# Two layers on one core: sums of squares and block products handed to GpSimd and ScalarE, new places and buffers in layer 0

## The chip, the core and the metric

The kernel runs on one core of a Trainium2 chip. The core has five engines with queues of their own: TensorE (PE, matrix products and transposes, results in PSUM), VectorE (DVE), ScalarE (ACT), GpSimd (POOL) and SyncE (SP, which issues DMAs; POOL issues DMAs too, the indirect ones among them). Each engine takes its instructions in order, and one that waits for a semaphore holds up all that stand behind it in its queue. The metric is the device time of one execution in microseconds, the median of several.

## What is computed

Two transformer layers over x of shape 8 x 512 x 256 in float32, each with a modulated LayerNorm, attention, a second LayerNorm and a mixture of experts. Layer 0's attention is a recurrence over time, and its experts take one of eight by argmax. Cut to what the change touches:

```python
def _L0_attn_ref(x, Wq, Wk, Wv, Wo, Wbeta, rms_weight):
    q = _l2_normalize(silu(x @ Wq.T).reshape(B, S, N, H))      # 16 heads of 16
    k = _l2_normalize(silu(x @ Wk.T).reshape(B, S, N, H))
    v = silu(x @ Wv.T).reshape(B, S, N, H)
    beta = jax.nn.sigmoid(x @ Wbeta.T)
    def step(M, inp):
        q_t, k_t, v_t, b_t = inp
        out_t = jnp.einsum('bnh,bnhd->bnd', q_t, M)
        retrieved = jnp.einsum('bnhd,bnd->bnh', M, k_t)
        M = M + b_t[..., None, None] * jnp.einsum('bnh,bnd->bnhd', k_t, v_t - retrieved)
        return (M, out_t)
    ...                                                          # scan over the 512 steps
    out = out / rms * rms_weight
    return out @ Wo.T

def _L0_ffn_ref(x, gate_w, gate_b, expert_bias, w1, b1, w2, b2):
    top_idx = jnp.argmax(gate_logits, axis=-1)
    for e in range(NUM_EXPERTS):
        h = jax.nn.relu(x @ w1[e] + b1[e])
        out = out + (top_idx == e) * (h @ w2[e] + b2[e])

h = _layernorm(x) * (1 + ca) + sa
x = x + ga * _L0_attn_ref(h, ...)
h = _layernorm(x) * (1 + cb) + sb
x = x + gb * _L0_ffn_ref(h, ...)
...                                # layer 1: softmax attention with a bias, dense weighted experts
```

## The kernel before

The 512 times are cut into four tiles of 128 (`NT`); a tile holds 128 times of all eight batches, with time on the partitions, 256 values a batch.

**Layer 0.** `scan(i, K, V)` runs the recurrence of tile i on VectorE, 128 steps one after the other, with the 8 x 16 states on the partitions and 16 x 16 of M along the row. A step is four dependent operations: product L625, reduction L629, outer product L635, subtraction L640; every eight steps come L621 and L631. It yields after each step. `run(pieces, steps)` sorts pieces of other work by a place, a number, and issues each when the scan has come to the step of that number; pieces with a place behind the last step, and all pieces when no scan runs, are issued in the order of their places. `tc.issue_after(step)` puts the instructions of a piece behind that step on VectorE's queue; the other engines get them in the order in which they are issued.

Three kinds of work run beside scan s:

- `front(s+1)`, from place 47 on (30 in scan 0): `stats`, `normal`, `turn`, `project` for each batch, where ScalarE writes q, k, v, beta and the squares of q and k (L533); `squares` sums them in groups of 16 (L537, VectorE); per half of the batches `roots` (ScalarE takes square roots of the sums, L550) and `scales` (VectorE from L554, then the products L572, POOL); `heads` turns k and v for the scan.
- `attend(s-1)`, from place 0 on: per batch `turn`, `scores`, `mask` (POOL, L725), `weigh`, `state`, `project`. `state` takes the batch's part of the state for the next tiles out of PSUM, zeroed outside the heads' blocks by a product with `block` on VectorE (L797 for tile 0, L800 for later ones), and adds it (L801, POOL). Per half come `roots` (L804, VectorE), `rest` (scaling on ScalarE, L808, product and sum on POOL, L811 and L812, and the store of x1, L813) and `stats` (L820).
- `follow(s-1)` adds the routing and the experts of that tile. `route` is a generator of six pieces at places 38, 47, 56, 61, 63, 65: it normalises the rows in place (L870), turns them, makes the logits (L893, added to the bias in L908), turns them back into the same rows (`h[b]`), counts rows by expert (L928, L933, L940, L948) and ends with `slot` and `idx` (L980) and eight scatters to `hs` by indirect DMA (L984). `experts` has 15 slots of 128 rows, each of two halves: weights by indirect DMA on POOL (L1005, two buffers per part), rows `hslot` from `hs`, first product L1032, ReLU L1041, second product L1050, the bias L1056, and the store L1057 to `ys`. The first ten or twelve slots are issued behind place 73 of the same scan (`late`, `pace`); the rest go by `starts` into the next scan, or, for tile 2, into the tail. Then `gather` fetches each batch's rows of `ys` (L1065), multiplies them by the gate (L1094) and adds them to x in DRAM (L1095, an accumulating DMA), through the rotating buffers `yrow` (two).

After scan 3 comes the tail: the rest of tile 2's slots, the attention and routing of tile 3, the gathers of tiles 0 and 1, then tile 3's fifteen slots one every ten places (the list `last`), with the gathers of tile 2 and pieces of layer 1's `prologue` between them at places 102 + 4k (L261 are its products for q and k). `place1` makes layer 1's buffers first, with two memsets on VectorE.

**Layer 1** follows: softmax attention (L1243 to L1290) and dense experts (L1402 to L1418).

Pool tags matter: tiles of one tag share its buffers, and a new tile waits for the readers of the old one. `terms`, `upd` and `K` belong to the scan, `dm` to `state`, `qT` (two buffers) is shared by `attend`'s q and by the squares.

Of the kernel before, what the change touches and what calls it, by code (L numbers as in the profile page):

```python
# [19 lines left out]
P = 128  # L20
B = 8
# [42 lines left out]
def tile_two_layers(ctx: ExitStack, tc: tile.TileContext, t: dict, out: bass.AP):  # L64
# [217 lines left out]
    with ExitStack() as l0:  # L282
# [167 lines left out]
        def front(i, at):  # L450
# [83 lines left out]
                got["sq", b] = sq  # L534

            def squares(b):
                nc.vector.tensor_reduce(  # L537
                    ss[:, :, b, :], got["sq", b].rearrange("p s (n d) -> p s n d", d=HD),
                    AX.X, ALU.add,
                )  # L540


            n = B if i == 0 else B // 2
# [98 lines left out]
        def attend(i, qk, V, x1, norms):  # L642
# [149 lines left out]
            def state(b):  # L792
                pm = got["pm", b]
                pmv = pm[:, :D].rearrange("p (g m) -> p g m", g=2)
                blocks = block.unsqueeze(1).to_broadcast([P, 2, P])
                if i == 0:
                    nc.vector.tensor_mul(bdM[:, b], pmv, blocks)  # L797
                else:
                    dm = ap.tile([P, 2, P], F32, tag="dm", name=f"dm{i}_{b}")
                    nc.vector.tensor_mul(dm, pmv, blocks)  # L800
                    nc.gpsimd.tensor_add(bdM[:, b], bdM[:, b], dm)  # L801

            def roots(h):
# [42 lines left out]
        def route(i, h, norms):  # L846
# [12 lines left out]
                return x.unsqueeze(1).to_broadcast([P, n, x.shape[1]])  # L859

            lg = grid("lg")
            for half in range(2):
                rs, off = scale_offset(fp, "f", *norms[half])
                pl = bank()
                turned = None
                for n in range(5):
                    b = 4 * half + n
                    if n < 4:
                        hb = h[b]
                        nc.scalar.activation(  # L870
                            hb, hb, AF.Identity, bias=off[:, n : n + 1], scale=rs[:, n : n + 1]
                        )
                        pt = bank()
                        for c in range(2):
                            nc.tensor.transpose(
                                pt[:, c * P : (c + 1) * P], hb[:, c * P : (c + 1) * P], ident
                            )
                        hT = fp.tile([P, 2, P], F32, tag="hTf", name=f"hTf{i}_{b}", bufs=2)
                        for c in range(2):
                            by, plus = scale[0][:, 1, c, b : b + 1], shift[0][:, 1, c, b : b + 1]  # L880
                            if i == NT - 1 and c == 1:
                                nc.vector.tensor_scalar(
                                    hT[:, c, :], pt[:, c * P : (c + 1) * P], by, plus,
                                    ALU.mult, ALU.add,
                                )
                            else:
                                nc.scalar.activation(
                                    hT[:, c, :], pt[:, c * P : (c + 1) * P], AF.Identity,
                                    bias=plus, scale=by,
                                )  # L890
                    if n > 0:
# [8 lines left out]
                                back[:, c * P : (c + 1) * P], turned[:, c, :], ident  # L900
                            )
                        if i == NT - 1:
                            nc.vector.tensor_copy(h[b - 1], back[:, :D])
                        else:
                            nc.scalar.copy(h[b - 1], back[:, :D])
                    turned = hT
                yield
                nc.vector.tensor_add(  # L908
# [83 lines left out]
        def experts(i, slot, idx):  # L992
# [79 lines left out]
            if i == NT - 1:  # L1072
# [9 lines left out]
                        nc.gpsimd.dma_start(x2d[b][i], rows[b], accum_op=ALU.add)  # L1082
                yield
                return
            queue = []
            for b in range(B + 1):
                if b < B:
                    yr = fp.tile([P, D], F32, tag="yrow", name=f"yrow{i}_{b}", bufs=2)
                    with tc.issue_after(issued["scatter" if i == NT - 2 else "fetch"]):
                        gather(b, yr)  # L1090
                    queue.append(yr)
                if b > 0:
                    yr = queue.pop(0)
                    nc.gpsimd.tensor_mul(yr, yr, gates[1][:, b - 1, :])  # L1094
                    nc.gpsimd.dma_start(x2d[b - 1][i], yr, accum_op=ALU.add)  # L1095
                yield

        def follow(i, qk, V):
# [16 lines left out]
            def on():  # L1115
                next(work["experts"])

            pieces += [(38, begin), (47, more), (56, more), (61, more), (63, more), (65, settle)]

            late, pace, starts = {  # L1120
                NT - 1: (0, 4, [10 * j for j in range(NSLOT)]),
                NT - 2: (12, 4.3, [58, 68, 71]),
                NT - 3: (10, 4.6, [10, 26, 44, 50, 66]),
            }.get(i, (10, 4.6, [10, 26, 42, 58, 70]))
            rest = []
            for j in range(NSLOT):
                for half in range(2):
                    if j < late:
                        pieces.append((73 + pace * (j + half / 2), on))
                    else:  # L1130
                        rest.append((starts[j - late] + 3 * half, on))
# [438 lines left out]
```

## Time and profile before

Three runs: 2272.21 us median, 2269.37 to 2276.05. The profiled execution took 2273.54 us, its span is 2271.8.

| engine | busy, us | share of the span |
|---|---|---|
| PE | 1747.4 | 77% |
| DVE | 1602.2 | 71% |
| ACT | 1063.0 | 47% |
| POOL | 646.9 | 28% |

| stretch, us of the span | what runs | length, us |
|---|---|---|
| 0 to 65 | loads, front of tile 0 | 65 |
| 65.2 to 319.4 | scan 0 | 254.1 |
| 321.2 to 587.2 | scan 1 | 266.0 |
| 589.1 to 867.7 | scan 2 | 278.6 |
| 869.6 to 1120.6 | scan 3 | 251.0 |
| 1120.6 to 1404 | tail of layer 0 | 283 |
| 1404 to 2272 | layer 1 | 868 |

The scans are cut at their first and last VectorE operation. The shares of busy time over the span say little here, since each stretch has its own full engine. The chain of waits on the profile's page covers only layer 1, so that the stretches before it have to be read from the slices, from windows over each of them and from the waits of the engine that is full there. A line of a group has line, engine and operation, tiles and shapes, the count, busy time, mean duration in ns, and the idle time before these instructions with what ended it. A line of waits has the waiting instruction, what released it, the sum in us, how many times and the longest. A line of windows has the window, then busy time and number of instructions for each engine named in the header, the granted clock, DMA's share and GB/s.

### The profile page before, as it was taken

How to read it: one execution, taken by the hardware profiler on the slowest of the kernel's cores; microseconds unless marked ns; L12 is line 12 of the kernel's file. 1: busy time of each engine (PE TensorE's matmuls, PEld its weight loads, DVE VectorE, ACT ScalarE, POOL GpSimd, SP SyncE). 2: the span in 40 equal slices, each digit the busy share in tenths (PEclk: the TensorE clock that was granted, in tenths of full speed). 3: DMA queues.
4: the chain of work that ended last, by engine and by line, in shares of the span. 5: the costliest groups of instructions: out<-in, count | busy, mean ns of one | idle time of the engine just before them, and what ended most of it. 6: DMA issues, size and time to landing. Idle time of an engine off the chain costs nothing. (4 is left out here: it accounts for less than half of the span.)

```text
span 2271.8 us, 32168 instructions
## 1 busy us (share of the span) xinstructions
PE 1747.4 (77%) x10874; PEld 1204.0 (53%) x10874; DVE 1602.2 (71%) x4609; ACT 1063.0 (47%) x2571; POOL 646.9 (28%) x795
## 2 busy tenths in 40 slices
PE   5233026669687896869796787899999999999997
PEld 3212024448566685658775676555555555555553
DVE  3899999889997899999653001676676767666654
ACT  5144024554355543533332233878475666647431
POOL 1102016144472544743326643000102011110111
PEclk9667567689887998979997899899999999999998
DMA  5110000167313583238956884100101010100001
GB/s 160 47 44 9 0 1 10 36 214 278 142 54 98 198 292 121 80 110 317 268 120 162 278 309 141 42 8 15 19 15 24 15 27 12 24 13 13 17 17 17
DMA packets 88628, 214.11 MB, mean 94 GB/s; under 512 B 10872, under 2 KB 64288, under 8 KB 72848
## 3 DMA queue, kind: packets, MB, share of 16 engines
q0 software_dynamic: 33696, 161.98, 22.3%
q1 hardware_dynamic: 54768, 50.09, 7.6%
q8 instruction: 86, 1.41, 0.3%
q14 instruction: 78, 0.64, 0.1%
HBM read 175.10 MB, written 36.93 MB: 93 GB/s over the span
## 5 line engine op out<-in xcount | busy, mean ns | idle before, releaser
L1257 ACT ACTIVATE pr<-sc,low 128x384 f32<-128x384 f32 (+3 forms) x512 | 255.6, 556 | 196.5 <-DVE low L1252 194.2
L1032 PE MATMUL ps<-hTs,w 128*128 128x128 f32 x1920 | 250.7, 293 | 47.6 <-ACT hTs L1024 32.9
L1252 DVE CUSTOM_DVE_ANT_0 sc<-ps,strips 128x384 f32<-128x384 f32 (+3 forms) x512 | 225.4, 485 | 86.7 <-PE ps L1243 55.0
L1032 PEld LDWEIGHTS ps<-hTs,w 128*128 128x128 f32 x1920 | 239.2, 206 | 62.0 <-ACT hTs L1024 48.1
L629 DVE TENSOR_REDUCE state<-terms 128x16 f32<-128x272 f32 x512 | 227.3, 444 | 15.5
L1050 PE MATMUL ps<-w,act 128*128 128x256 f32 x960 | 223.3, 387 | 15.4 <-DMA w<-in_wrows,idx 12.6
L1408 PE MATMUL ps<-ew,hTd 128*128 128x512 f32 x512 | 232.9, 608 | 0.0
L640 DVE TENSOR_TENSOR state<-state,upd 128x256 f32<-128x256 f32 x511 | 220.6, 432 | 17.2
L635 DVE TENSOR_TENSOR upd<-K,state 128x256 f32<-128x256 f32 x511 | 213.9, 419 | 14.9
L1041 ACT ACTIVATE act<-ps,w 128x128 f32<-128x128 f32 x480 | 137.2, 369 | 186.1 <-PE ps L1032 104.7
L625 DVE TENSOR_TENSOR terms<-state,K 128x256 f32<-128x256 f32 x512 | 214.6, 419 | 11.9
L1050 PEld LDWEIGHTS ps<-w,act 128*128 128x128 f32 x960 | 182.1, 194 | 41.1 <-issue 13.9
L1269 PE MATMUL ps<-cst,pr 128*128 128x128 f32 x1280 | 191.5, 295 | 15.2 <-DVE low L1252 12.9
L1413 DVE SCALAR_TENSOR_TENSOR accd<-ps,wtd,accd 128x256 f32<-128x256 f32 x256 | 123.7, 483 | 101.4 <-PE ps L1408 89.5
L1269 PEld LDWEIGHTS ps<-cst,pr 128*128 128x128 f32 x1280 | 149.0, 148 | 83.9 <-DVE low L1252 24.7
L1417 POOL TENSOR_TENSOR accd<-accd,bc_g 128x256 f32<-128x256 f32 x32 | 23.2, 725 | 563.7 <-DVE accd L1413 563.7
L1408 PEld LDWEIGHTS ps<-ew,hTd 128*128 128x128 f32 x512 | 96.4, 193 | 121.2 <-issue 107.6
L1005 POOL DMA_INDIRECT w<-in_wrows,idx x120 | 117.3, 977 | 122.8 <-ACT act L1041 89.7
L1243 PE MATMUL ps<-kT,qTc 32*128 32x384 f32 (+3 forms) x1024 | 131.5, 492 | 6.3 <-DVE low L1252 4.4
L1278 DVE COPY prT<-ps 128x512 f32<-128x512 f32 (+3 forms) x256 | 117.0, 484 | 10.3 <-PE ps L1269 9.9
L725 POOL TENSOR_TENSOR stk<-stk,cst 128x512 f32<-128x512 f32 x96 | 119.3, 1270 | 17.1 <-ACT stk L724 15.1
L1276 ACT COPY prT<-ps 128x512 f32<-128x512 f32 (+3 forms) x256 | 99.0, 414 | 8.6 <-PE ps L1269 8.2
(252 smaller groups left out, 2878.7 us busy)
## 6 DMA issues: line engine op xcount, KB each, us to landing
hs<-zero SPq DMA_DIRECT2D x4, 1920.0 KB
hslot<-hs SPq DMA_DIRECT2D x60, 128.0 KB
ys<-ysb POOLq DMA_DIRECT2D x60, 128.0 KB, 3.1
x<-in_x SPq DMA_DIRECT2D x32, 128.0 KB
strips<-strip_d SPq DMA_DIRECT2D x16, 256.0 KB
out<-accd POOLq DMA_DIRECT2D x32, 128.0 KB, 3.1
wm<-in_wmod SPq DMA_DIRECT2D x4, 768.0 KB
xt<-in_x SPq DMA_DIRECT2D x12, 256.0 KB
```

The lines of the kernel that those rows point to most:

```text
L625: nc.vector.tensor_mul(term[:, :, :HD], M, K[:, s, :].unsqueeze(1).to_broadcast([P, HD, HD]))
L629: nc.vector.tensor_reduce(delta, term, AX.X, ALU.add)
L635: nc.vector.tensor_mul(upd, K[:, s, :].unsqueeze(2).to_broadcast([P, HD, HD]), delta.unsqueeze(1).to_broadcast([P, HD, HD]),)
L640: yield nc.vector.tensor_sub(M, M, upd).ins
L1032: nc.tensor.matmul(ph[:, q * P : (q + 1) * P], w[:, k * FF + f * P : k * FF + (f + 1) * P], hT[:, k, :], start=(k == 0), stop=(k == 1),)
L1041: nc.scalar.activation(act[:, f, :], ph[:, q * P : (q + 1) * P], AF.Relu, bias=w[:, 2 * FF + f : 2 * FF + f + 1],)
L1050: nc.tensor.matmul(py[:, :D], act[:, f, :], w[:, f * D : (f + 1) * D], start=(f == 0), stop=(f == NFC - 1),)
L1243: made = nc.tensor.matmul(pscs[r][:, :W], qT[rows, g, o, i * P : (i + 1) * P], kT[rows, g, :W], start=True, stop=True,)
L1252: nc.vector.tensor_tensor_reduce(out=sc[:, :W], in0=pscs[r][:, :W], in1=strips[:, n, S - W :], scale=1.0, scalar=3.0e38, op0=ALU.add, op1= ...
L1257: nc.scalar.activation(pr, sc[:, :W], AF.Exp, bias=low, scale=-1.0)
L1269: nc.tensor.transpose(pt[:, (i - j) * P : (i - j + 1) * P], prs[r, i][:, j * P : (j + 1) * P], ident,)
L1408: nc.tensor.matmul(pe, hT[0][:, k, cols], ew[:, k, e : e + 2, :], start=(k == 0), stop=(k == 1),)
```

## The change

- The sums of squares of tiles 1 to 3 are no longer one VectorE reduction but four additions in place on POOL, which halve the groups of 16; their pieces stand three places later, `roots` and `scales` four, `heads` three.
- The block product of the state is a copy out of PSUM on ScalarE and a product with the blocks in place on POOL.
- Tiles 0 and 1: routing at other places (38, 49, 59, 65, 69, 72), `rest` and `stats` of the second half two places later, its `roots` four; the first experts' slot at 77 (tiles 0, 1) in place of 73, and other places for the rest of the slots.
- The gathers of tiles 0 and 1 go into one buffer of eight rows (tag `K`) and are issued three rows ahead of product and addition; tile 2 keeps two buffers and one row.
- In the last tile the normalised rows go to buffers of their own (tags `upd` and `dm`) and the rows turned back to `h_last` (tag `terms`), from which the scatters read.
- The pieces k = 6 and 7 of layer 1's prologue go to places 151 and 152. As built, `place1`'s two memsets come behind the last tile's `idx` on VectorE's queue.

```diff
             def squares(b):
-                nc.vector.tensor_reduce(
-                    ss[:, :, b, :], got["sq", b].rearrange("p s (n d) -> p s n d", d=HD),
-                    AX.X, ALU.add,
-                )
+                if i == 0:
...
+                    return
+                terms = got["sq", b].rearrange("p s (n d) -> p s n d", d=HD)
+                for m in (HD // 2, HD // 4, HD // 8):
+                    nc.gpsimd.tensor_add(
+                        terms[:, :, :, :m], terms[:, :, :, :m], terms[:, :, :, m : 2 * m]
+                    )
+                nc.gpsimd.tensor_add(ss[:, :, b, :], terms[:, :, :, 0], terms[:, :, :, 1])
...
-                    pieces.append((at + 8 * p + 3 * c + 11, lambda b=b: squares(b)))
+                    pieces.append((at + 8 * p + 3 * c + (14 if i else 11), lambda b=b: squares(b)))
-                last = at + 16 * h + (23 if i else 39)
+                last = at + 16 * h + (27 if i else 39)
-            pieces.append((at + 46, lambda: heads("K", qk[:, 1])))
-            pieces.append((at + 49, lambda: heads("V", v)))
+            pieces.append((at + 49, lambda: heads("K", qk[:, 1])))
+            pieces.append((at + 52, lambda: heads("V", v)))
...
-                if i == 0:
-                    nc.vector.tensor_mul(bdM[:, b], pmv, blocks)
-                else:
+                dm = bdM[:, b]
+                if i > 0:
                     dm = ap.tile([P, 2, P], F32, tag="dm", name=f"dm{i}_{b}")
-                    nc.vector.tensor_mul(dm, pmv, blocks)
+                nc.scalar.copy(dm, pmv)
+                nc.gpsimd.tensor_mul(dm, dm, blocks)
+                if i > 0:
                     nc.gpsimd.tensor_add(bdM[:, b], bdM[:, b], dm)
...
-                pieces.append((20 * h + 27, lambda h=h: roots(h)))
+                wait = 2 * h if i < NT - 2 else 0
+                pieces.append((20 * h + 27 + 2 * wait, lambda h=h: roots(h)))
                 for b in range(4 * h, 4 * h + 4):
-                    pieces.append((18 * h + 28 + b, lambda b=b: rest(b)))
-                    pieces.append((16 * h + 32 + b, lambda b=b: stats(b)))
+                    pieces.append((18 * h + 28 + wait + b, lambda b=b: rest(b)))
+                    pieces.append((16 * h + 32 + wait + b, lambda b=b: stats(b)))
+        DEPTH = (3, 3, 1, 1)
...
+            xn, made = h, h
+            if i == NT - 1:
+                xn = [
...
+                room = ap.tile([P, STEPS, HD, HD + 1], F32, tag="terms", name="h_last")
...
+                made = [room[:, b * D : (b + 1) * D] for b in range(B)]
...
-                        hb = h[b]
+                        hb = xn[b]
                         nc.scalar.activation(
-                            hb, hb, AF.Identity, bias=off[:, n : n + 1], scale=rs[:, n : n + 1]
+                            hb, h[b], AF.Identity, bias=off[:, n : n + 1], scale=rs[:, n : n + 1]
                         )
...
-                            nc.vector.tensor_copy(h[b - 1], back[:, :D])
+                            nc.vector.tensor_copy(made[b - 1], back[:, :D])
...
-                    in_=h[b],
+                    in_=made[b],
...
+            if i < NT - 2 and "fetched" not in w1:
+                fetched = ap.tile([P, P, HD], F32, tag="K", name="fetched")
+                w1["fetched"] = fetched.rearrange("p t d -> p (t d)")
             queue = []
-            for b in range(B + 1):
+            for b in range(B + DEPTH[i]):
                 if b < B:
-                    yr = fp.tile([P, D], F32, tag="yrow", name=f"yrow{i}_{b}", bufs=2)
+                    if i < NT - 2:
+                        yr = w1["fetched"][:, b * D : (b + 1) * D]
+                    else:
+                        yr = fp.tile([P, D], F32, tag="yrow", name=f"yrow{i}_{b}", bufs=2)
...
-                if b > 0:
-                    yr = queue.pop(0)
-                    nc.gpsimd.tensor_mul(yr, yr, gates[1][:, b - 1, :])
-                    nc.gpsimd.dma_start(x2d[b - 1][i], yr, accum_op=ALU.add)
+                if b >= DEPTH[i]:
+                    yr, k = queue.pop(0), b - DEPTH[i]
+                    nc.gpsimd.tensor_mul(yr, yr, gates[1][:, k, :])
+                    nc.gpsimd.dma_start(x2d[k][i], yr, accum_op=ALU.add)
...
-            pieces += [(38, begin), (47, more), (56, more), (61, more), (63, more), (65, settle)]
-            late, pace, starts = {
-                NT - 1: (0, 4, [10 * j for j in range(NSLOT)]),
-                NT - 2: (12, 4.3, [58, 68, 71]),
-                NT - 3: (10, 4.6, [10, 26, 44, 50, 66]),
-            }.get(i, (10, 4.6, [10, 26, 42, 58, 70]))
+            places = (38, 49, 59, 65, 69, 72) if i < NT - 2 else (38, 47, 56, 61, 63, 65)
+            pieces += zip(places, (begin, more, more, more, more, settle))
+            first, late, pace, starts = {
+                NT - 1: (0, 0, 4, [(10 * j, 10 * j + 3) for j in range(NSLOT)]),
+                NT - 2: (73, 12, 4.3, [(54, 64), (66, 67), (68, 69)]),
+                NT - 3: (77, 10, 4.6, [(9, 12), (22, 25), (35, 38), (58, 61), (70, 73)]),
+                NT - 4: (77, 10, 4.6, [(8, 11), (20, 23), (32, 35), (60, 63), (67, 70)]),
+            }[i]
...
-                        pieces.append((73 + pace * (j + half / 2), on))
+                        pieces.append((first + pace * (j + half / 2), on))
...
-            return pieces, rest, [(at + apart * n, on) for n in range(B + 1)]
+            return pieces, rest, [
+                (at + apart * n, on) for n in range(B + DEPTH[i])
+            ]
...
-            last.append((102 + 4 * k if k < NT + 4 else 201 + k, piece))
+            place = 102 + 4 * k if k < NT + 2 else 145 + k if k < NT + 4 else 201 + k
+            last.append((place, piece))
```

More of the change, by code (lines that the diff above doesn't have):

```diff
@@ L536, in squares @@
             def squares(b):
-                nc.vector.tensor_reduce(
-                    ss[:, :, b, :], got["sq", b].rearrange("p s (n d) -> p s n d", d=HD),
-                    AX.X, ALU.add,
-                )
+                if i == 0:
+                    nc.vector.tensor_reduce(
+                        ss[:, :, b, :], got["sq", b].rearrange("p s (n d) -> p s n d", d=HD),
+                        AX.X, ALU.add,
+                    )
[4 more added lines that the diff above has]
+                        terms[:, :, :, :m], terms[:, :, :, :m], terms[:, :, :, m : 2 * m]
+                    )
+                nc.gpsimd.tensor_add(ss[:, :, b, :], terms[:, :, :, 0], terms[:, :, :, 1])
             n = B if i == 0 else B // 2
@@ L861, in route @@
             lg = grid("lg")
+            xn, made = h, h
+            if i == NT - 1:
+                xn = [
+                    ap.tile([P, HD, HD], F32, tag="upd", name=f"xnf{b}").rearrange(
+                        "p a b -> p (a b)"
+                    )
+                    if b % 2
+                    else ap.tile([P, 2, P], F32, tag="dm", name=f"xnf{b}").rearrange(
+                        "p a b -> p (a b)"
+                    )
+                    for b in range(2)
+                ] * (B // 2)
+                room = ap.tile([P, STEPS, HD, HD + 1], F32, tag="terms", name="h_last")
+                room = room.rearrange("p s a b -> p (s a b)")
+                made = [room[:, b * D : (b + 1) * D] for b in range(B)]
             for half in range(2):
@@ L902, in route @@
                         if i == NT - 1:
-                            nc.vector.tensor_copy(h[b - 1], back[:, :D])
+                            nc.vector.tensor_copy(made[b - 1], back[:, :D])
                         else:
-                            nc.scalar.copy(h[b - 1], back[:, :D])
+                            nc.scalar.copy(made[b - 1], back[:, :D])
                     turned = hT
@@ L1128, in follow @@
                     if j < late:
-                        pieces.append((73 + pace * (j + half / 2), on))
+                        pieces.append((first + pace * (j + half / 2), on))
                     else:
-                        rest.append((starts[j - late] + 3 * half, on))
+                        rest.append((starts[j - late][half], on))
             if i == NT - 1:
```

## The prediction

> **What bounds the kernel now.** I read the page's slices first, then the stages, then the waits of the engine that is full in each.
>
> ```profile
> PE   5233026669687896869796787899999999999997
> DVE  3899999889997899999653001676676767666654
> POOL 1102016144472544743326643000102011110111
> ```
>
> A slice is 56.8 us. In slices 2 to 20 DVE is near full: the four scans. Slices 21 to 25 have no full engine: the tail of layer 0. From 26 on PE is full: layer 1, whose order this change leaves as it is, so I take nothing from there. The stages, cut at the scans' ends:
>
> ```profile
> core 0: us, PE busy (x) PEld busy (x) DVE busy (x) ACT busy (x) POOL busy (x), PEclk, DMA share, GB/s
> 320.00:588.00 268.00, 188.24 (x1214) 147.57 (x1214) 243.25 (x634) 132.40 (x324) 116.50 (x140) 0.80 0.39 135
> 588.00:869.00 281.00, 226.70 (x1530) 185.90 (x1529) 244.22 (x634) 142.94 (x371) 134.88 (x164) 0.89 0.44 154
> 869.00:1121.00 252.00, 197.34 (x1459) 168.68 (x1458) 232.48 (x592) 99.96 (x295) 121.68 (x141) 0.89 0.51 171
> 1200.00:1300.00 100.00, 72.93 (x424) 65.31 (x424) 13.82 (x45) 27.88 (x90) 66.58 (x76) 0.82 0.74 224
> ```
>
> Scan 2 is longer than scan 3 by 29 us though DVE is busy only 12 us more in it: the rest is waiting. In the tail POOL has 67 of 100 us, DMA 0.74, PE 73: a chain through several engines. DVE's waits over the four scans:
>
> ```profile
> DVE ss L537 <- ACT sq L533: 12.0, 2, 6.4
> DVE ms L804 <- ACT ms L789: 11.4, 4, 7.0
> DVE lg L908 <- PE ps L893: 5.4, 2, 3.0
> DVE count L933 <- PE ps L928: 3.3, 2, 2.8
> DVE over L948 <- PE ps L940: 1.0, 1, 1.0
> DVE stf L820 <- POOL x L812: 0.5, 1, 0.5
> ```
>
> That is 33.6 us: 9.1 in scan 1, 21.1 in scan 2, 3.4 in scan 3. So a scan is paid for by what DVE executes, plus these stops.
>
> **Work taken off DVE.** Both moved kinds, over the scans:
>
> ```profile
> L537 DVE TENSOR_REDUCE ss<-sq 128x32 f32<-128x512 f32 x24 | 16.2, 675 | 12.1 <-ACT sq L533 12.0
> L800 DVE TENSOR_TENSOR dm<-ps,cst 128x256 f32<-128x256 f32 x16 | 6.6, 412 | 0.0
> L797 DVE TENSOR_TENSOR bdM<-ps,cst 128x256 f32<-128x256 f32 x8 | 3.3, 411 | 0.0
> ```
>
> An undisturbed step is 1.858 us. In the timeline a step that holds an L537 is 0.47 us longer, one with an L797 or L800 0.21: the rest of their busy time falls into gaps between the scan's four dependent operations. So 24 x 0.47 = 11.2 and 24 x 0.21 = 5.0: **-16.1 us** (3.8 of it in scan 0). Ends: nothing if the gaps took all, -26.1 if all their busy time counts. I take the measured steps.
>
> **What takes it over.** ACT gets 24 copies of 128x256 out of PSUM; its nearest row, L786, takes 373 ns, and ACT is busy at most 143 of 281 us in a scan: hidden, 3 us a scan if it weren't. POOL's two-tensor rows are 1.27 us for 512 elements (L725) and 0.73 for 256 (L811), so 0.19 + 2.1 ns an element. A batch's four halvings (256, 128, 64, 32 elements) cost 0.73 + 0.46 + 0.32 + 0.26 = 1.77 us, 14.2 a tile; a tile's eight products 8 x 0.73 = 5.9. POOL goes from 117, 135 and 122 us in scans 1 to 3 to about 137, 155 and 128 (scan 3 has no squares). Room on average; not always in order, which the next part takes up.
>
> Does busy POOL slow DVE? Two windows of L635, one of the scan's products, the first with POOL idle (0 of 36 us), the second with POOL busy 18.27 of 20:
>
> ```profile
> 425.00:461.00 36.00, 5.85 (x14) 0.78 0.24 69
> 649.00:669.00 20.00, 3.79 (x10) 1.00 0.42 146
> ```
>
> 418 and 379 ns apiece (the window cuts one), and the steps are 1.858 us long under POOL's products as without them. So no charge. A rule speaks against that: the Trainium skill, "SBUF — State Buffer", section "SBUF: two separate sides", says that VectorE and GpSimd share one pair of ports as an exclusive lock, held for a whole instruction, also against a VectorE operation with two SBUF inputs. By it the 60 us that POOL gains here (42.5 + 17.7) could come back on the scan, and the sum below would be about 2285 us; this trace does not agree, and the row decides.
>
> **The waits in the scans after.** Scan 2, by cause. L804 of the second half (7.0) waited for a projection that stood behind slot 12 of tile 0's experts on PE, at step 42; now the slot is at 32 and the reciprocal four steps (7.5 us) later: gone. The router's pieces go 2 to 9 steps (4 to 17 us) later and had waits of 2.4, 2.8 and 1.0: gone. The squares' wait (6.4) moves: DVE no longer waits for ACT's Square but, in the scales (L554), for POOL's sums. On POOL the sums of the last batch stand behind 8 scatters (1.3 us each), the block of L572 products and the fetches of slots 3 and 4 (L1005), and a fetch waits until ACT has read the buffer of the slot before it. Counting slots at 8.07 us on PE from the routing on, I get the sums 50 to 54 us after the indices, where DVE asks for them after 40: 10 to 15, ends 0 and 27 (one and a half slots more). Against 21.1 I take 13. Scan 1: same queue, one slot earlier: 5 (ends 0 and 15) in place of 5.6, the router's 3.5 gone, a new wait of 0 to 5 on PE in the last router piece: 7 (0 to 20) against 9.1. Scan 3: its attention pieces are not moved, and at 930 to 950 POOL is busy 18.3 of 20 us, so two products more there (1.6 us) make the reciprocals later: 5 (1 to 9) against 3.4. Sum 25 for 33.6: **-8.6 us**, ends -33 and +22. What waits with DVE when it stops is the scan itself, nothing else.
>
> **The tail.** After scan 3 POOL's queue holds the 16 gathers of tiles 0 and 1, with two row buffers:
>
> ```profile
> POOL yrow L1094 <- DMA yrow<-ys,slot: 28.7, 10, 9.8
> POOL yrow L1065 <- DMA x<-yrow: 27.3, 15, 8.8
> ```
>
> A gather waits until the row before last was added out to DRAM, a product until its gather landed. They run from 1132.4 to 1232.4, 100 us, and behind them come a fetch and tile 3's scatters:
>
> ```profile
> 1238.82 5.84 PE L1032 MATMUL ps<-hTs,w 128*128 128x128 f32 x32 [8.40 <-DMA w<-in_wrows,idx]
> ...
> 1254.53 0.69 PE L1020 MATMUL ps<-cst,hslot 128*128 128x128 f32 x2 [6.41 <-DMA hslot<-hs]
> ```
>
> With eight rows and three gathers ahead neither wait is left (landing takes 3.5 us in the median, three rows' work 10): 1.3 + 1.0 + 1.3 us a row, 16 x 3.6 = 58 us, done near 1192. Then the routing decides, whose indices are ready at 1225.2. It sat behind two memsets (about 4 us) and, on PE, behind slot 12 (6 to 8 us), which can now fill PE's idle 11.6 us before 1205.5: indices at 1213 to 1215. Scatters 10.4 us, plus the 7.3 us that lay between their end and the first rows on PE: tile 3's first slot at 1236 to 1238 for 1254.5, -17. The two L261 pieces (2 x 3.63 us on PE) go behind tile 3's experts, into PE's wait of 10.1 us for the last rows: -7.3; without that cover, 0. The last tile's extra buffers cost no instruction. **-24 us**, ends -32 (experts closer to PE's pace, too) and -6 (transfers, at a DMA share of 0.74, set the pace whenever the slots begin).
>
> **Sum.** -16.1 - 8.6 - 24 = -48.7 on the profiled execution's 2273.5 (span 2271.8): 2224.8. The median of the runs shown lies 1.3 lower: **2224 us**.
>
> **The rivals.**
> - *The tail is paced by transfers.* The gathers finish early and tile 3's weights still come no sooner. For it: DMA at 0.74; against it: in the chain above what ends PE's waits is POOL issuing late. 2273.5 - 16.1 - 8.6 - 6 = 2243.
> - *POOL's order becomes the bound (the slower side).* Place: the scales of scans 1 and 2, behind a fetch that waits for a slot's activations, with ACT's last Square itself behind that slot. Price: 8 us for each slot that the sums fall behind; three slots more in each of the two scans is 48, and POOL's late products in scan 3 another 4, with a tail that gives 6: 2273.5 - 16.1 - 8.6 + 52 - 6 = 2295. It decides from waits of about 80 us in the scans, against 33.6 now and 25 expected. For it: POOL at 0.91 in places, in order; against it: the slots come at 8 us and the slack of each piece is 4 us and more.
> - *More vanishes than I take.* The scans' waits fall to 5 and the tail reaches its end: 2273.5 - 16.1 - 28.6 - 32 = 2197.
> - *The moved work was hidden anyway*: the gaps took all of it. Then -8.6 - 24: 2241; the longer steps under L537 speak against it.
>
> **How the numbers follow.** Forecast (2205 to 2240) 0.55; paced by transfers 0.14; POOL's order 0.14; more vanishes 0.10; hidden anyway 0.07. The range 2194 to 2262 leaves out the worst of POOL's order and the far ends. Within 0.3% (2265 to 2279) is about what a measurement can't tell from no change; only the milder part of POOL's order lies there: 0.05. Slower 0.12, faster 0.83.
>
> **What would show it.** Scan 0 some 4 us shorter, steps with a former L537 at 1.86 us; waits of DVE at the scales of 5 and 13 us with POOL as releaser, L804 of scan 2 without its 7 us; POOL's 16 gathers in about 60 us and tile 3's first slot 115 to 118 us after the scans instead of 134; layer 1 unchanged. Wrong it would be if the scans' waits grew past 40 us, if PE still waited for weights in the tail while POOL is idle, or if the scan's steps grew under POOL's new work.

## The result and the profile after

The changed kernel takes 2286.28 us in the median (2275.43 to 2292.61, 11 runs), the kernel before on the same chip 2269.37 (2261.01 to 2277.12, 11 runs): a ratio of 1.0069, 95% interval 1.0048 to 1.0090. It is slower, where 2224 us and faster had been forecast.

The profiled execution of the changed kernel took 2279.0 us, its span is 2277.3: 5.5 us longer than that of before. By stage, cut at the first scan products and at VectorE's first operation on a score of layer 1, below called the first score (us; scan 3 ends and the tail begins with the end of the last reduction):

| stage | before | after | difference |
|---|---|---|---|
| scan 0 | 256.0 | 252.1 | -3.9 |
| scan 1 | 267.9 | 262.3 | -5.6 |
| scan 2 | 280.5 | 293.8 | +13.3 |
| scan 3 | 251.4 | 264.9 | +13.5 |
| tail to the first score | 299.0 | 293.9 | -5.1 |
| layer 1 from there | 852.2 | 845.5 | -6.7 |

The medians are 17 us apart and these two executions 5.5: the profiled one of after lies 7 us below its median, that of before 4 above. A scan's length is the same to 3.5 us in the four profiles with the places of the changed kernel, and to 6 us in the five with the moved work and the places of before; layer 1, whose order is the same in all kernels here, took between 842.7 and 854.4.

The windows over scans 1 to 3 of the changed kernel (columns as in the table of windows of before):

```profile
core 0: us, PE busy (x) PEld busy (x) DVE busy (x) ACT busy (x) POOL busy (x), PEclk, DMA share, GB/s
316.80:579.10 262.30, 180.68 (x1178) 141.06 (x1177) 235.65 (x617) 132.63 (x323) 131.56 (x176) 0.80 0.36 123
579.10:872.90 293.80, 229.17 (x1553) 187.77 (x1552) 237.91 (x617) 148.62 (x388) 154.80 (x206) 0.87 0.43 151
872.90:1137.80 264.90, 199.12 (x1467) 170.66 (x1466) 230.02 (x583) 102.66 (x304) 130.34 (x153) 0.86 0.51 172
```

The work did move: POOL has 155 us in scan 2 for 135, and DVE's busy time is down to 238 from 244. But scan 2 now lasts 56 us longer than DVE is busy. DVE's waits over the four scans of the changed kernel:

```profile
DVE ss L563 <- ACT ss L559: 21.9, 2, 13.8
DVE ms L814 <- ACT ms L798: 17.5, 4, 7.3
DVE lg L937 <- PE ps L922: 10.0, 2, 5.8
DVE count L962 <- PE ps L957: 9.1, 2, 5.3
DVE stf L830 <- POOL x L822: 3.9, 3, 1.9
DVE rsa L132 <- ACT sda L126: 3.1, 2, 1.8
DVE rsf L132 <- ACT sdf L126: 1.8, 1, 1.8
DVE over L977 <- PE ps L969: 1.5, 2, 0.8
```

L563 is the scales, L814 the reciprocal behind the projections, L937, L962 and L977 the router. Their sum is 68.8 us, against 33.6 before: 10.7, 39.7 and 18.5 in scans 1, 2 and 3. That is 35 us more waiting; the scans less their waits are 18 us shorter (1004.3 for 1022.2). One of the waits in its place, TensorE's timeline in scan 3 (start, us, line, tiles; in brackets idle time and what ended it):

```profile
1006.36 5.95 PE L1061 MATMUL ps<-hTs,w 128*128 128x128 f32 x32
1012.15 3.62 PE L1079 MATMUL ps<-w,act 128*128 128x256 f32 x16
1015.70 0.43 PE L957 MATMUL ps<-cst,pick 128*64 128x128 f32 x2
```

The router's count (L957, 0.4 us) stands behind a whole expert slot (L1061 and L1079, 9.3 us), which the new starts put there; VectorE stops for 5.3 us until it is done.

### The profile page after: what moved, and what is told of

It reads as the page before. It is cut to its first block, busy times and chain, and to the rows that moved or that the text cites. A ratio compares the mean times of both kernels' runs of the same rounds, so it can differ in the third digit from the quotient of the medians.

```text
span 2277.3 us, 32234 instructions
## 1 busy us (share of the span) xinstructions
PE 1738.7 (76%) x10874; PEld 1195.8 (53%) x10874; DVE 1584.2 (70%) x4561; ACT 1071.2 (47%) x2596; POOL 703.1 (31%) x915
## 5 line engine op out<-in xcount | busy, mean ns | idle before, releaser
L1061 PE MATMUL ps<-hTs,w 128*128 128x128 f32 x1920 | 249.3, 292 | 46.4 <-ACT hTs L1053 40.2
L1061 PEld LDWEIGHTS ps<-hTs,w 128*128 128x128 f32 x1920 | 237.9, 205 | 61.7 <-ACT hTs L1053 55.0
L1079 PE MATMUL ps<-w,act 128*128 128x256 f32 x960 | 227.8, 392 | 16.6 <-DMA w<-in_wrows,idx 13.3
L644 DVE TENSOR_TENSOR upd<-K,state 128x256 f32<-128x256 f32 x511 | 214.0, 419 | 14.8
L1079 PEld LDWEIGHTS ps<-w,act 128*128 128x128 f32 x960 | 184.8, 197 | 42.5 <-issue 12.2
L1284 PE MATMUL ps<-kT,qTc 32*128 32x128 f32 (+3 forms) x1024 | 131.1, 486 | 4.2 <-DVE low L1293 2.6
## 6 DMA issues: line engine op xcount, KB each, us to landing
strips<-strip_d SPq DMA_DIRECT2D x16, 256.0 KB
xt<-in_x SPq DMA_DIRECT2D x12, 256.0 KB
```

Source lines behind the costliest of these rows:

```text
L644: nc.vector.tensor_mul(upd, K[:, s, :].unsqueeze(2).to_broadcast([P, HD, HD]), delta.unsqueeze(1).to_broadcast([P, HD, HD]),)
L1061: nc.tensor.matmul(ph[:, q * P : (q + 1) * P], w[:, k * FF + f * P : k * FF + (f + 1) * P], hT[:, k, :], start=(k == 0), stop=(k == 1),)
L1079: nc.tensor.matmul(py[:, :D], act[:, f, :], w[:, f * D : (f + 1) * D], start=(f == 0), stop=(f == NFC - 1),)
L1284: made = nc.tensor.matmul(pscs[r][:, :W], qT[rows, g, o, i * P : (i + 1) * P], kT[rows, g, :W], start=True, stop=True,)
```

## The experiments

Each kernel is the changed one or the one before with the edit named; times are given as ratios to the kernel before on the same chip, stages and waits from one profiled execution of each. Two theories were held against each other from the first: A, that places and buffers cost the time and the moved work gives what was forecast; B, that GpSimd's queue, with its new work, is what VectorE waits for.

### One part undone each

The squares' sums on VectorE again, they and what follows them at the places of before (`in ()` is never true):

```diff
-                if i == 0:
+                if i not in ():
                     nc.vector.tensor_reduce(
...
-                    pieces.append((at + 8 * p + 3 * c + (14 if i else 11), lambda b=b: squares(b)))
+                    pieces.append((at + 8 * p + 3 * c + (14 if i in () else 11), lambda b=b: squares(b)))
-                last = at + 16 * h + (27 if i else 39)
+                last = at + 16 * h + (27 if i in () else 23 if i else 39)
...
```

> The changed kernel with one part undone: the sums of squares of tiles 1 to 3 are VectorE reductions again, at the places of before. The changed kernel's profile has scans of 251.7, 262.0, 293.5 and 263.9 us (before 255.7, 267.5, 280.2, 250.5). Theory A (places and buffers cost the time; the squares give what was forecast): scan 0 goes back to 255.7; in scans 1 and 2 the waits at the scales (8.1 and 13.8 us) turn into waits for ScalarE's Square of about 6 each, and 3.8 of work comes back: scan 1 264, scan 2 290, scan 3 unchanged at 264; whole about 2 to 4 us slower or equal. Theory B (POOL's order): without the squares' additions POOL is never late, VectorE's waits in scan 2 fall by more than 20 us to some 18, the whole is over 10 us faster than the changed kernel.

Ratio 1.0053 (1.0023 to 1.0083). Scans 256.1, 266.9, 287.2, 267.5: scan 0 as A expected, scans 1 and 3 some 3 longer, scan 2 3 shorter. The waits are 59.1 us against 68.8, not the fall by 20 that B asked for: with GpSimd's sums gone, VectorE stops for 18.2 us at the squares instead, for ScalarE's Square.

The block product on VectorE again:

```diff
-                nc.scalar.copy(dm, pmv)
-                nc.gpsimd.tensor_mul(dm, dm, blocks)
+                nc.vector.tensor_mul(dm, pmv, blocks)
```

> The changed kernel with the block product of the state undone: one VectorE product out of PSUM, as before. Theory A: 24 products come back at 0.21 us (5.0 us), the waits for the projections (L814: 4.8, 7.3, 3.0, 2.4 us) stay, because TensorE is late there: scans 1, 2, 3 at 263.7, 295, 265.6; about 5 us slower than the changed kernel. Theory B: the projections are late because ScalarE's copy waits for the single buffer that POOL's product and addition hold; then those waits fall from 17.5 to the 11.4 of before or less, scans 2 and 3 lose 3 to 8 us each, and the whole is some 5 us faster.

Ratio 1.0023 (1.0002 to 1.0044). Scans 252.1, 263.5, 293.0, 265.4. The waits for the projections stay (16.7 of 17.5 us), which is A's forecast; the 5 us that A expected to come back were 0.9 in the scans, because the waits fell by some 4 in all. But the edit doesn't settle B, as GpSimd's addition still holds the single buffer `dm`: VectorE's product now waits for it, 6.0 us in three stops that neither the changed kernel nor the one before has. In the changed kernel it is ScalarE's copy that waits, here over the four scans:

```profile
ACT dm L808 <- POOL bdM L811: 51.9, 11, 10.3
```

Its longest stop, in scan 2 until 656.3, holds up a projection on TensorE:

```profile
657.04 2.07 PE L782 MATMUL ps<-wo,oT 128*128 128x256 f32 x4 [7.22 <-ACT oT L771]
```

ScalarE's copy `oT` (L771), for which this projection waits, stands right behind that copy of `dm`. What part of VectorE's waits for the projections comes of this, this run doesn't tell.

All places back, everything else as changed:

```diff
-                wait = 2 * h if i < NT - 2 else 0
+                wait = 0
...
-            places = (38, 49, 59, 65, 69, 72) if i < NT - 2 else (38, 47, 56, 61, 63, 65)
+            places = (38, 47, 56, 61, 63, 65)
...
-                NT - 2: (73, 12, 4.3, [(54, 64), (66, 67), (68, 69)]),
-                NT - 3: (77, 10, 4.6, [(9, 12), (22, 25), (35, 38), (58, 61), (70, 73)]),
-                NT - 4: (77, 10, 4.6, [(8, 11), (20, 23), (32, 35), (60, 63), (67, 70)]),
+                NT - 2: (73, 12, 4.3, [(58, 61), (68, 71), (71, 74)]),
+                NT - 3: (73, 10, 4.6, [(10, 13), (26, 29), (44, 47), (50, 53), (66, 69)]),
+                NT - 4: (73, 10, 4.6, [(10, 13), (26, 29), (42, 45), (58, 61), (70, 73)]),
```

> The changed kernel with all places of routing, statistics and expert slots put back as before (the places of the squares' sums and what follows them stay). Theory A: in scan 3 the waits of the router's pieces (5.8 and 5.3 us) and in scan 2 (4.3 and 3.7) fall to those of before or to nothing, the scans to about 262 (1), 283 (2) and 254 (3); the tail keeps its length; whole 15 to 20 us faster than the changed kernel, about 2265. Theory B: the waits stay where they are, POOL's work being the same: within 5 us of the changed kernel.

Ratio 0.9892 (0.9846 to 0.9939), median 2250.4. The scans are 252.1, 256.1, 270.2, 258.7: 1037.0 in sum against 1073.1 changed and 1055.8 before. More than A expected. The waits of this kernel over the scans:

```profile
DVE ms L814 <- ACT ms L798: 14.3, 3, 6.1
DVE lg L937 <- PE ps L922: 6.4, 3, 3.2
DVE ss L563 <- ACT ss L559: 5.3, 1, 5.3
DVE count L962 <- PE ps L957: 4.4, 2, 3.4
```

The four and the small ones beside them come to 33.9 us. That is before's sum (33.6): with the places of before, the new work on GpSimd and ScalarE adds no waiting in sum. It moves it: before's 12.0 us at the squares are 5.3 at the scales, but the projections take 14.3 us for 11.4, and scan 3 waits 12.4 us for 3.4. B in its plain form, that the new work makes VectorE wait wherever its places are, is out; what the places do by way of GpSimd's order comes below.

The last tile's rows in place again:

```diff
             xn, made = h, h
-            if i == NT - 1:
+            if False:
```

> The changed kernel with the last tile's rows in place again (no buffers from the scan's tags for them); gathers, places and the rest as changed. Theory A: the load of layer 1's expert weights, which in the changed kernel starts only after tile 3's scatters and in front of its first row load (that load takes 14.3 us to issue, TensorE waits 14.5 us), goes back to some 82 us after the scans; tile 3's first slot begins about 120 us after the scans instead of 136; scans unchanged (1072 us in sum); whole about 15 us faster than the changed kernel. Theory B: the tail is paced by POOL and transfers; the first slot stays at 134 to 137 us and the time within 4 us.

Ratio 1.0013 (0.9986 to 1.0040). Neither expectation holds in full. The load of the expert weights does go back, from 112 to 86 us after the scans, but tile 3's indices are ready 13.7 us later (112.3 against 98.6), and its first slot begins at 134.3 instead of 135.1. So the new buffers bring the routing forward and the load that they hold back takes it away again. The changed kernel's SyncE queue and TensorE there:

```profile
1250.00 1.01 SPq L212 DMA_DIRECT2D ew<-in_expert_w  x2
1251.12 14.29 SPq L1046 DMA_DIRECT2D hslot<-hs  x1
```

```profile
1272.92 0.69 PE L1049 MATMUL ps<-cst,hslot 128*128 128x128 f32 x2 [14.46 <-DMA hslot<-hs]
```

The scan's buffers `terms`, `upd` and `dm` used to be free when the scan ended, and `place1` takes their room for layer 1, `ew` (2.1 MB by its shape, 2 x 8 x 256 values on 128 partitions) among it. With the last rows in them the load waits for the scatters, and then stands right in front of the rows that TensorE needs.

### Which places, and the load alone

The load behind tile 3's first rows, once with all places back and once with the changed places:

```diff
-        for k in range(2):
-            nc.sync.dma_start(
-                ew[:, k], t["expert_w"][:, k * P : (k + 1) * P, :].rearrange("e p d -> p e d")
-            )
...
+        def load_ew():
+            for k in range(2):
+                nc.sync.dma_start(
+                    w1["ew"][:, k],
+                    t["expert_w"][:, k * P : (k + 1) * P, :].rearrange("e p d -> p e d"),
+                )
+        last.append((145, load_ew))
```

> The changed kernel with all places put back (as in the run of all places, 2250 us, scans 1037 us in sum) and the load of layer 1's expert weights issued late, at place 145, behind the last expert slots. Theory A: that load stood in front of tile 3's first rows (14 us of TensorE's waiting); without it tile 3's first slot begins 120 to 123 us after the scans instead of 134, and the whole is 10 to 14 us faster, about 2238. Theory C: scatters and weight fetches set that moment, the slot begins at 131 us or later and the time stays within 4 us of 2250.

> The changed kernel, all its places kept, with that load alone moved to place 145. Theory A: indices at 99 us after the scans as before, TensorE's wait of 14.5 us for the first rows goes, first slot at about 120 to 122 us; scans unchanged at 1073 us; about 2274, 10 to 14 us faster than the changed kernel. Theory C: within 4 us of it.

With all places back: ratio 0.9846 (0.9802 to 0.9890), median 2238.7. The first slot begins at 125.0 us (134.4 without this edit), the first score comes at 287.7 (295.7). With the changed places: the slot at 122.9 (135.1), the first score at 284.9 (293.9); but ratio 1.0045 (1.0023 to 1.0066), for 1.0069 (1.0048 to 1.0090) of the changed kernel: not the 10 to 14 us that A expected. In its profile scan 3 is 3.5 and layer 1 9 us longer than in the changed kernel's. Theory A holds for the moment of the slot, which moves by 9 and 12 us; what of it reaches the first score is 8 to 9 us. On SyncE's queue the load follows the first rows in both kernels, earlier than its place says; why, no run shows. TensorE's first rows of tile 3 in the first of the two kernels:

```profile
1227.26 0.44 PE L1044 MATMUL ps<-cst,hslot 128*128 128x128 f32 x2 [4.88 <-DMA hslot<-hs]
```

The places in two halves: only the starts of the left-over slots put back (the last three lines of the diff above without their first numbers), and only routing, statistics and first slots put back (the rest of it).

> The changed kernel with only the starts of the left-over expert slots put back (steps 10, 26, 42 or 44 and so on in scans 2 and 3, 58, 68, 71 in the tail); routing, statistics and the first slot stay at the new places. Theory A (two causes, by TensorE's and by GpSimd's order): scan 1 stays 262 with its 8 us at the scales, scan 2 falls from 294 to about 282 as the waits for the projections and the router's logits go, scan 3 from 265 to 259; whole about 15 us faster than the changed kernel. Rival: the starts don't matter, the routing's places do: scans 2 and 3 stay at 290 and above, 263 and above.

> The changed kernel with only routing, statistics and the first expert slot of tiles 0 and 1 put back to the places of before, the new starts kept. Theory A: the scatters and the first fetches come 7 steps earlier on GpSimd's queue and the squares' sums are not late: the wait at the scales falls from 8.1 to 0 in scan 1 and from 13.8 to about 5 in scan 2; scan 1 at 256, scan 2 at 283 to 288, scan 3 unchanged at 265; whole some 14 us faster than the changed kernel. Rival: the sums wait for something else, the waits at the scales stay above 6 and 11.

Starts back: ratio 0.9976 (0.9955 to 0.9997), scans 252.1, 262.4, 282.6, 259.1. Routing back: 0.9997 (0.9967 to 1.0027), scans 252.1, 256.2, 277.9, 267.4. So the starts cost 16.9 us of scan (11.2 in scan 2, 5.8 in scan 3), the later routing 19.6 (6.1 in scan 1, 15.9 in scan 2, 2.5 given back in scan 3); together 36.5, and both undone gave 36.1. They are two causes, and over the scans they add (in a single scan they miss the sum by up to 3.5 us). The second is a group: later routing, later statistics and the later first slot were put back together. The waits of the two kernels, first the one with the old starts, then the one with the old routing:

```profile
DVE ss L563 <- ACT ss L559: 22.3, 2, 13.9
DVE ms L814 <- ACT ms L798: 20.6, 4, 6.8
DVE count L962 <- PE ps L957: 4.7, 1, 4.7
DVE lg L937 <- PE ps L922: 2.8, 1, 2.8
```

```profile
DVE lg L937 <- PE ps L922: 18.2, 4, 6.1
DVE ms L814 <- ACT ms L798: 14.6, 3, 6.5
DVE count L962 <- PE ps L957: 8.3, 3, 4.8
DVE ss L563 <- ACT ss L559: 3.5, 1, 3.5
```

The scales (L563) stop for 22 us with the new routing whatever the starts, and for 3.5 to 5.3 with the old one. The router (L937, L962) stops for 19.1 us (changed kernel) and 26.5 with the new starts and for 7.5 and 10.8 (all places back) with the old ones. The projections (L814) stop for 17.5 and 20.6 us with the new routing and for 14.6 and 14.3 with the old one. How the routing reaches the scales can be read on POOL's timeline in the changed kernel's scan 2, around the last batch's sums (L546 and L549):

```profile
801.61 0.71 POOL L546 TENSOR_TENSOR sq<-sq 128x256 f32<-128x256 f32 x1
802.48 0.97 POOL L1034 DMA_INDIRECT w<-in_wrows,idx  x1 [0.16 <-issue]
...
804.34 0.45 POOL L546 TENSOR_TENSOR sq<-sq 128x128 f32<-128x128 f32 x1
...
806.68 0.30 POOL L546 TENSOR_TENSOR sq<-sq 128x64 f32<-128x64 f32 x1
809.20 0.95 POOL L1034 DMA_INDIRECT w<-in_wrows,idx  x1 [2.22 <-ACT act L1070]
810.16 0.26 POOL L549 TENSOR_TENSOR ss<-sq 128x32 f32<-128x32 f32 x1
```

The four additions need 1.7 us and take 8.8, because three fetches and a slot's addition and store stand between them, and the last fetch waits 2.2 us for a slot's activations. VectorE asks for the result at 798.4 and has it at 812.1. The rest of this stop is ScalarE's: 2.8 us until it has squared the batch, and 1.4 us between the last sum and its roots (L559), which stand behind the copy of a slot's result. With the routing 7 steps earlier that stop is 3.5 us.

### The moved work alone, and the parts of the tail

The two moved kinds of work alone, all else as before (the first two parts of the change's diff):

> The kernel before with only the two moved kinds of work: the squares' sums as halvings on GpSimd (with their later places) and the block product as ScalarE copy and GpSimd product; all other places, the gathers, the last tile's rows and the prologue as before. Theory A (the work moved off VectorE counts by its steps and brings no more waiting): scans 1036 to 1040 us in sum against 1056, waits about 34 us as before, tail and layer 1 as before; about 17 us faster than before, ratio 0.992. Theory B (GpSimd's order): VectorE's waits grow to 45 or more and the ratio is 0.998 or above.

Ratio 0.9930 (0.9901 to 0.9960). Scans 252.0, 257.2, 274.7, 256.5, 1040.5 in sum, waits 36.4 us: A's numbers for the scans but for some 2 us of waits. The forecast's -16.1 us for the work is 15.3 here, as length of the scans. A's tail is not as before: in this profile it takes 306.2 us to the first score for 299.0, with TensorE busy 241.9 us for 233.8 over nearly as many products (1666 for 1660), at a mean granted clock of 0.86 for 0.89. Whether the clock alone made it longer isn't shown.

On the kernel with places back and the load late: the gathers of tiles 0 and 1 through two rotating buffers again; the prologue's pieces back between the slots; the block product on VectorE.

```diff
-        DEPTH = (3, 3, 1, 1)
+        DEPTH = (1, 1, 1, 1)
...
-                    if i < NT - 2:
+                    if False:
                         yr = w1["fetched"][:, b * D : (b + 1) * D]
```

> The kernel with all places put back and the expert weights' load late (2239 us, tile 3's first slot 125 us after the scans), with the gathers of tiles 0 and 1 through two rotating buffers again. Theory A: the sixteen gathers take about 100 us again and hold up the weight fetch and tile 3's scatters behind them; first slot at 132 to 136 us, about 8 us slower. Rival: the routing decides that moment and the gathers are hidden; slot at 123 to 127, time within 4 us.

Ratio 0.9884 (0.9839 to 0.9930). The first slot at 136.1 us for 125.0, the first score at 297.9 for 287.7. The indices were there at 99.2, earlier than the 107.0 of the kernel with the quick gathers, and yet the scatters came at 118 instead of 107: they stand behind the gathers, the last addition of which goes out at 112.7 us (83.2 with eight rows). POOL's waits in this tail:

```profile
POOL yrow L1089 <- DMA x<-yrow: 31.3, 14, 11.0
POOL yrow L1125 <- DMA yrow<-ys,slot: 23.4, 10, 7.9
```

```diff
-            place = 102 + 4 * k if k < NT + 2 else 145 + k if k < NT + 4 else 201 + k
+            place = 102 + 4 * k if k < NT + 4 else 201 + k
```

> The same kernel with the two prologue pieces of layer 1 (8 L261 products each, 2 x 3.63 us) back between tile 3's slots at places 126 and 130. Theory A: TensorE is the bound there and idle at the end; experts end 277 us after the scans instead of 270, first score of layer 1 at 293 to 295 instead of 288; 5 to 7 us slower. Rival: transfers set the pace of those slots and the pieces lie in their waits; first score within 2 us.

Ratio 0.9890 (0.9842 to 0.9939). From first slot to the end of the experts 151.0 us against 145.0: 6.0 of the 7.3 expected. The first score comes only 2.8 later, the slots having begun 2.9 earlier.

> The same kernel with the block product of the state as one VectorE product again. Theory A: VectorE gets 5.0 us of work back; in scans 2 and 3 the projections' waits (7.1 and 9.6 us) fall by as much or more, since ScalarE no longer waits for the buffer that GpSimd's product and addition hold: waits of 3 to 5 in scan 3 as before; scans 1034 to 1040 in sum, time within 4 us. Rival: those waits have nothing to do with it; scans 1041, 5 us slower.

Ratio 0.9817 (0.9770 to 0.9864), median 2239.3. Scans 1041.6 in sum against 1036.3 to 1043.1 in the five profiles with the product moved and the old places; the waits for the projections are 10.8 us against 14 to 18. The product as copy and GpSimd work gives VectorE 5 us and takes about as much back in waits: nothing either way that these runs can tell. The squares' sums alone, with the places of before, weren't run.

## Why the prediction was wrong, point by point

- **Work off VectorE, -16.1 us: right.** Alone it took 15.3 us off the scans' length, with 2.8 more of waits; with old places 18.8, at unchanged waits; scan 0 lost 3.9 for the 3.8 forecast. Less right is "hidden" for ScalarE's copies: they wait 52 us over the scans for the buffer that GpSimd holds, and with old places the 5.0 us of the block product aren't seen in the scans' length. Steps carry no charge for a busy POOL: L644, the outer product, is 419 ns as before.
- **The waits in the scans, -8.6 us: the step that failed.** They grew by 35.2: 9.9 at the squares and scales, 10.9 at the router, 6.1 at the projections, 8.3 at the statistics. With the old places nothing of this growth is left in the sum (33.9). The prediction took each wait by itself, moved its place later and called it gone: "now the slot is at 32 and the reciprocal four steps (7.5 us) later: gone", measured 7.3; "The router's pieces go 2 to 9 steps (4 to 17 us) later ... gone", measured 4.2, 3.7 and 0.7 in scan 2. For the router it didn't ask what else the new starts put on TensorE ahead of those pieces: three left-over slots in the first 35 steps in place of two, and in scan 3, whose router wasn't moved, one right in front of the logits and one in front of the count (5.8 and 5.3 us, none forecast). The projections' 7.3 isn't explained by the starts, which leave it at 6.5 when put back; ScalarE's 10.3 us behind `dm` and the router's work on TensorE come before it, but no run takes it apart. The scales were sized well, 8.1 and 13.8 for 5 and 13; but that is what the later routing makes of them, and the prediction priced it as the cost of the sums on POOL. With the old routing it is 0 in scan 1 and 0 to 6.7 in scan 2 (seven profiles).
- **The tail, -24 us: 5.1 came.** The gathers do nearly what was said (65 us from the first gather to the last addition, for 58; 18.0 us of waiting for them are left, where none was forecast, as they land after 11.4 us in the median and not 3.5) and are worth 10 us at the first score when nothing else is late. The indices come 98.6 us after the scans for the 92 to 94 forecast: slot 12, meant to fill TensorE's gap, waits 10.9 us for its rows and then runs ahead of the routing. The first slot, forecast at 115 to 118 us, begins at 135.1. 12 us of that lie in the sentence "The last tile's extra buffers cost no instruction": they cost a release, and with it the place of a 2.1 MB load; with this load alone moved the slot begins at 122.9. The prologue's -7.3 is 6.0.
- **The rivals.** The slower one named POOL's order at the scales and put 80 us of waits as the point of decision; 68.8 came, with 21.9 there. Its sign was right and its mechanism a third of it, set off by the later routing; much of the rest is TensorE's order, which no rival had. That transfers pace the tail is half true: one transfer in the wrong place held up the first slot; no run tested their rate. The prediction's sum with the port lock, about 2285, lies next to the 2286 measured by chance: the scan's operations take the time they took before.

The medians differ by 17 us and the two profiles by 5.5. Scans and tail together are 12.2 us longer in the profile of after, and layer 1, which the change leaves as it is, 6.7 shorter. Its length goes with the granted clock: among all fourteen profiles it is longest (854.4 and 852.2, the kernel before) at a mean clock of 0.96 and shortest (842.7) at 0.98. Whole times do the same: among the executions of the kernel before on each of three chips (25, 25 and 14), time and mean clock have a correlation of -0.82 to -0.90. What sets the clock stays open.

The kernel with all places back and the load late beats both, 0.9846 and, with the block product on VectorE, 0.9817 of the time before; the intervals of these two overlap.

## What to carry to other kernels

Work taken off a full engine counts by how much longer the steps were that held it, and here that could be had with the waits the same in sum; places that are tuned to one order should be moved one group at a time, since two groups here cost 17 and 20 us of scan and hid a gain of 15 to 19. When a piece is moved earlier, list what it now stands in front of on every queue: a half-microsecond operation behind a nine-microsecond block is the wait. When a buffer is lent to a later use, look for what waits for its room, a large load above all.

## What the runs showed of the chip

GpSimd's two-input operations and VectorE's scan operations ran side by side without a trace of each other: in the changed kernel the 110 of L644's 511 products that lie to 95% or more under a GpSimd operation of this kind take 419 ns in the mean, and so do the 340 that none touches, as L635 did before. The port lock that the prediction took from the Trainium skill's page "SBUF — State Buffer" (section "SBUF: two separate sides") does not show here. Layer 1, the same instructions in the same order, took 842.7 us in one profile and 854.4 in another, at mean granted clocks of 0.98 and 0.96 over that stretch; a tail gain of 9 us can disappear in that.
